# Input tiles of 96 neighbouring partitions, loaded ahead of the small constants, and one product of a step with 112 weight columns

## The chip, the cores and the metric

The kernel runs on one core of one Trainium2 chip, in float32. The metric is the device time of one execution in microseconds (us), as a median of several runs. The engines are TensorE (PE, with its weight loads listed as PEld), VectorE (DVE), ScalarE (ACT), GpSimd (POOL) and SyncE (SP, which here only issues DMA transfers).

## The reference

The input x has 32 images of 48 channels, 64 rows and 128 columns. Two layers follow one another. Each normalises x in 16 groups of three channels (GroupNorm without weights), passes the result through four recurrent scans, and adds x. A scan adds to each row (or column) a convolution of five taps of the row before it:

```python
def step(w, b):
    def f(carry, inp):
        nxt = inp + _conv1d(carry, w, b)      # 48 -> 48 channels, 5 taps
        return (nxt, nxt)
    return f
...
x = x + conv(_gn(x), down_w, down_b, right_w, right_b, left_w, left_b)   # twice
```

The first two scans run down and up the rows (both with the down weights), the last two right and left along the columns. Each step needs the one before it.

## The kernel before

**Groups and phases.** The 32 images are four groups of eight. A rows phase does the downward and upward scan of one group (126 steps), a columns phase the rightward and leftward scan of two groups (254 steps). There are twelve phases (PHASES) and 2024 steps, in one fixed order: rows of group 0, rows of group 1, columns of both, rows of group 2, and so on, for both layers.

**A step.** Eight neighbouring columns and 48 channels make 384 values, which lie as three blocks of 128 partitions (PIECES says which column offset e and which channels lie where). A row is then three blocks of 128 x 128 values: 16 column octets of eight images. The five taps reach from a block into the neighbouring ones, so a step is nine products (PRODUCTS, L63 to L73), of which two reach over the edge of an octet ("border" products, with 96 weight columns, BORDER). `step` (L710) issues them at L723; after the last product of a block the vector engine adds bias and input (L732) and so makes the next row. Each float32 product is two matmul records in the profile, so a step has 18.

**The order of work.** Every engine executes its instructions in the order in which the program issues them (`in_order`, L231). Around the steps, an agenda (`at`, L800) places other work at a step number: loads, row moves, scaling, statistics. `starts` holds the step at which each phase begins. What comes before the first step, and part of what runs during the first steps, is written out by hand in `first_group` (L1003 to L1129). All DMA transfers go out through `dma` (L226), on SP's queue if no other is given.

**Group 0's start.** `take_batch` loads x in two parts of rows, each part in a tile of 112 partitions: 48 channels of one run of 16 rows at partitions 0 to 47, 48 channels of the next 16 rows at partitions 64 to 111 (SIDES). The 16 partitions between are set to zero (L1035). Each image and side is a transfer of its own. From these tiles come three things:

- Statistics: DVE's bn_stats and bn_aggr (L395, L398), then in `scaling` (L289) products with a mask matrix that average over the three channels of a group and both sides (L300) and spread the result to the 128-partition layout (L311, with maskp), and the coefficients scale and offset (L351 to L374).
- Rows 0 to 7: `rows_by_product` (L1055) lets PE move the values into the three-block layout by products with pieces of an identity matrix (L1061); ACT copies the results out of PSUM (L1068). The identity pieces are cut from a tile in DRAM, `ident`, by small transfers into the space of the weights that are needed later.
- All other rows: `permute` (L544) rearranges a row of both sides on POOL (some quarters on ACT), `put_out` writes it to a DRAM tensor (xin), `move_rows` (L571) reads it back into the three-block layout, ten transfers for eight rows with runs of 128 bytes, and `scale_rows` (ACT, L596) or `scale_at_once` (DVE or POOL, L607) normalises it.

Between the loads of x, `let_go` mixes the small loads that were held back: the taps and weights (`load_weights`), the masks and biases (`load_constants`), and the identity pieces. `spread_masks` (L279) makes maskp and scales mask_in, which is used for the statistics of results later.

**Groups 1 to 3.** `plan_input` (L815) places the loads (`take_in`), permutes, puts and statistics (on ACT, `take_others`) of the other groups at steps of the agenda. Group 1's first load comes at the end of `first_group`, after the reads of group 0's rows. `plan_rows` (L835) places row moves and scalings.

Of the kernel before, what the change touches and what calls it, by code (L numbers as in the profile page):

```python
# [33 lines left out]
C = 48  # L34
ODD = 64
P = ODD + C
TAPS = 5
# [4 lines left out]
GB = 8  # L42
# [26 lines left out]
    (1, 2, 0),  # L69
    (0, 1, 0),  # L70
    (1, 1, 0),
    (2, 1, 0),
)  # L73
BORDER = 2 * C

# [43 lines left out]
def kernel(  # L119
# [57 lines left out]
    mask_sb = const([P, P], "mask_sb")  # L177
    maskp = const([P, NG, FULL], "maskp")
    mask_in = const([FULL, NG, P], "mask_in")
# [92 lines left out]

    def load_constants(dma):
        dma(mask_sb, mask)
        for e, c0, c1, o, p0 in PIECES:
            dma(bd[p0 : p0 + c1 - c0, o], bias[c0:c1])
            dma(mask_in[p0 : p0 + c1 - c0, o], mask[c0:c1])

    def spread_masks():  # L279
        for e, c0, c1, o, p0 in PIECES:  # L280
            nc.gpsimd.tensor_copy(maskp[:, o, p0 : p0 + c1 - c0], mask_sb[:, c0:c1])

        nc.gpsimd.tensor_scalar(mask_in, mask_in, 2.0 / E8, None, ALU.mult)
# [5 lines left out]
    def scaling(key, layer, g, averages, masks, slack=0):  # L289
# [29 lines left out]
        average(ps[0:P, 0], mean_p)  # L319
        if n == 1:  # L320
            expand(ps[:, 1 : 1 + NG], mean_p[:, 0])
# [3 lines left out]
        dev = spare[0 : FULL if n > 1 else P, 0:n]  # L325
        if n > 1:
            mean_c = stat_tile([P, GB], "mean_c", key)
            nc.vector.tensor_copy(mean_c, ps[0:P, 0])
            yield
            expand(ps[:, 1 : 1 + NG], mean_c)  # L330
            yield
            nc.vector.tensor_tensor(dev, mean_p, ps[:, 1 : 1 + NG], ALU.subtract)
        else:
            nc.vector.tensor_tensor(dev, mean_p, ps[0:P, 0:1], ALU.subtract)
        nc.vector.tensor_copy(mean, ps[:, 1 : 1 + NG])
        pool.tensor_tensor(dev, dev, dev, ALU.mult)
        yield
        for _ in range(slack):
            yield
        if n == 1:  # L340
            expand(ps[:, 2 + NG :], dev[:, 0], var_p[:, 0])
        else:
            average(ps[0:P, 1 + NG], dev, var_p)
            yield
            var_c = stat_tile([P, GB], "var_c", key)
            nc.vector.tensor_copy(var_c, ps[0:P, 1 + NG])
            yield
            expand(ps[:, 2 + NG :], var_c)
# [5 lines left out]
        nc.scalar.activation(std, var, AF.Sqrt)  # L354
        yield
        yield
# [20 lines left out]
    class InputStats:  # L377
# [3 lines left out]
        def __init__(self, key, nv):  # L381
            self.nv = nv
            self.mv = stat_tile([P, 1, GB, 2], "mv_x", key)
            if nv:
                self.st = stat_tile([P, nv, NBN * 6], "bn", key)
            if nv < GB:
                self.sum, self.neg, self.dev2 = (
                    stat_tile([P, GB, NBN], f"{n}_x", key)[:, nv:] for n in ("sum", "neg", "dev2")
# [11 lines left out]
        def take_others(self, i, nat):  # L400
            k = nat.shape[-1] // BN
            for square in (False, True):
                for b in range(self.nv, GB):
                    for n in range(k):
                        at = b - self.nv, slice(i + n, i + n + 1)
                        piece = nat[:, b, n * BN : (n + 1) * BN]
                        if square:
                            nc.scalar.activation(
                                junk[0:P],
# [5 lines left out]
                        else:  # L415
                            nc.scalar.activation(  # L416
                                junk[0:P],
# [8 lines left out]
        def __call__(self, key, slack):  # L426
# [3 lines left out]
            if self.nv < GB:  # L430
                n = GB - self.nv
                mean = stat_tile([P, GB], "mean_x", key)[:, 0:n]
# [6 lines left out]
                    dev, dev, mean.unsqueeze(2).to_broadcast([P, n, NBN]), ALU.add  # L439
# [7 lines left out]
                var = stat_tile([P, GB], "var_x", key)[:, 0:n]  # L447
# [74 lines left out]
    x_masks = [mask_sb]  # L522
    r_masks = [mask_in[:, g] for g in range(NG)]


    def take_in(g, h0, nat):

        n = nat.shape[-1] // W
        for s in range(2):
            h = h0 + s * n  # L530
            if n < E8:
                dma(
                    nat[SIDES[s]],
                    x[g * GB : (g + 1) * GB, :, h : h + n].rearrange("b c h w -> c b (h w)"),
                )
            else:
                for b in range(GB):
                    take_batch(g, b, h, s, nat)

    def take_batch(g, b, h, s, nat):  # L540
        n = nat.shape[-1] // W
        dma(nat[SIDES[s], b], x[g * GB + b, :, h : h + n].rearrange("c h w -> c (h w)"))
# [12 lines left out]
    def put_out(g, h, perm, stride):  # L555

        n = perm.shape[-1] // (W * GB)
        for s in range(2):
            dma(
                lines(source[0][g], h + s * stride, h + s * stride + n),  # L560
                perm[SIDES[s]].rearrange("p (m n) -> p m n", n=LINE),
            )
# [147 lines left out]
    def step(key, weights, b_at, src, inp, dst, whole, part):  # L710
# [8 lines left out]
        for i, o, s in PRODUCTS:  # L719
            seen[o] += 1  # L720
            m = BORDER if s else FULL
# [93 lines left out]
    def plan_input(g, times, work, lag, nats, perms):  # L815
# [5 lines left out]
        for j, t in enumerate(times):  # L821
# [3 lines left out]
            for i in range(per):  # L825
                perm, r = perms[i % len(perms)], i * rows // per
                at(t + i * work / per, permute, nat, r, perm, [nc.gpsimd])
                at(t + i * work / per + 4, put_out, g, 2 * rows * j + r, perm, rows)
            at(t + lag, stats.take_others, pieces_of * j, nat)
            if j + ahead < len(times):  # L830
                free = t + 7
                at(free, take_in, g, 2 * rows * (j + ahead), nat)
# [148 lines left out]
    def wide_nat(i0, n):  # L981
        return arena[0:P, i0 : i0 + GB * n * W].rearrange("p (b m) -> p b m", b=GB)

    tiles = [stage[0:P, i] for i in range(4)]
# [10 lines left out]

    at(starts[1] + 50, more_weights, "right", 0, RIGHT)
# [6 lines left out]
    def first_group():  # L1003
        later = []

        def hold(dst, src):
            later.append((dst, src))

        def let_go(n):
            for _ in range(min(n, len(later))):  # L1010
                dma(*later.pop(0))


        spare = {k: wt[k].rearrange("p i n -> p (i n)") for k in ("down1", "right", "left")}
        to_row = [spare["right"][0:C, i * FULL : (i + 1) * FULL] for i in range(9)]
        to_row += [spare["left"][0:C, 0:FULL]]
        one = last[0:C, 0 : C + 1]
        ident = dram.tile([C, C + 1], F32, tag="ident", name="ident")
        square = ident.rearrange("c n -> (c n)")[0 : C * C].rearrange("(c n) -> c n", n=C)

        def make_ident():
            dma(ident, one)
            for m, (e, c0, c1, o, p0) in zip(to_row, PIECES):
                hold(m[c0:c1, p0 : p0 + c1 - c0], square[c0:c1, c0:c1])
# [3 lines left out]
        nc.vector.memset(one, 0.0)  # L1028
        nc.vector.memset(one[:, 0:1], 1.0)
        for b in range(2 * GB):  # L1030
            if b == 2:
                nc.vector.memset(spare["right"], 0.0)
                nc.vector.memset(spare["left"], 0.0)
            i, b = divmod(b, GB)
            (nc.vector if b % 2 else nc.gpsimd).memset(parts[i][32:64, b], 0.0)  # L1035

        def take(i, b):
            for s in range(2):
                take_batch(0, b, i * HALF + s * rows, s, parts[i])

        stats = InputStats("x0", GB)
        perms = [spare["down1"][0:P, 0 : W * GB]]
        perms += [row_views(0)[0][0:P, o, 24:32].rearrange("p h n -> p (h n)") for o in range(NG)]
        more = [spare[k][0:P, 0 : W * GB] for k in ("down1", "right", "left")]
        more += [slot[2][0:P, i * W * GB : (i + 1) * W * GB] for i in range(4)]

        def permute_row(i, r, *engines):
            ring = more if i else perms
            permute(parts[i], r, ring[r % len(ring)], engines)

        def put_row(i, r):
            ring = more if i else perms
            put_out(0, i * HALF + r, ring[r % len(ring)], rows)

        def rows_by_product(h0, n):  # L1055
            src = parts[0][0:C].rearrange("p b (r k e) -> p e r k b", k=NK, e=E8)
# [16 lines left out]
        take(0, 0)  # L1073
        make_ident()
        for b in range(1, 3):
            take(0, b)
        load_weights("down0", 0, DOWN, hold)
        load_constants(hold)
        for b in range(3, GB):
# [125 lines left out]
```

## Time and profile before

| | |
|---|---|
| median of three runs | 4308.83 us (4308.38 to 4317.33) |
| profiled execution | 4311.88 us |
| its span in the profile | 4309.7 us |
| granted TensorE clock | 0.98 of full speed |
| first step starts at | 103.28 us |
| group 0's last row reads end at | 203.6 us |

A profile line of PE, DVE, ACT or POOL gives the line of the kernel, the engine, the operation, the output and input names, and the number of instructions, then their busy time and the mean of one in ns, then the idle time before them and what ended it. "L596 ... <-DMA arena<-xin 154.7" says that ACT's scaling at L596 stood idle for 154.7 us until DMA transfers from xin to the arena had landed. "SPq" is SP as the issuer of transfers. The page's costliest groups of instructions are, apart from the steps' products, ACT's row scaling (816 instructions, 576.0 us), POOL's permutes (458, 271.0 us at L553 into the arena) and the residual additions on POOL (80, 362.9 us). Over the whole span the DMA engines move 158 GB/s on average, 2,006,689 of 2,117,983 packets being under 512 bytes.

### The profile page before, as it was taken

What the parts mean: (1) busy time and instruction counts of PE and PEld (TensorE: products, weight loads), DVE (VectorE), ACT (ScalarE), POOL (GpSimd) and SP (SyncE); (2) the same over time, 40 slices, a digit from 0 to 9 for tenths busy, and PEclk for the clock granted to TensorE, in tenths of its full rate; (3) what the DMA queues carried; (4) which work ended last, traced back from release to release, by engine and by line L of the source; (5) the groups of instructions that cost most, each with busy time, mean ns of one, the idle gap of its engine ahead of it and who ended that gap; (6) DMA issues with size and microseconds to landing.
All of it is one profiled execution on the core that took longest, in us unless ns stands there. A gap on an engine that the chain in (4) does not pass through costs nothing. (4 is left out here: it accounts for less than half of the span.)

```text
span 4309.7 us, 90123 instructions
## 1 busy us (share of the span) xinstructions
PE 4080.8 (95%) x36672; PEld 4051.4 (94%) x36672; DVE 2161.1 (50%) x6508; ACT 1337.0 (31%) x2656; POOL 904.1 (21%) x906
## 2 busy tenths in 40 slices
PE   4898998999999999998999999999999999999992
PEld 1898998999999999998999999999999999999992
DVE  6344444446654454444446654444444444444443
ACT  1593301445784454200006772613000002110122
POOL 4571011325322020000005310000000024420352
PEclk9999999999999999999999999999999999999996
DMA  9999799877998999679507979929288039989999
GB/s 179 179 192 161 112 156 174 214 142 224 230 183 143 151 157 157 105 127 177 118 1 234 222 158 145 151 45 160 47 137 201 1 76 239 255 245 153 180 202 180
DMA packets 2117983, 680.34 MB, mean 158 GB/s; under 512 B 2006689, under 2 KB 2057409, under 8 KB 2077633
## 3 DMA queue, kind: packets, MB, share of 16 engines
q1 hardware_dynamic: 2019552, 582.30, 71.2%
q10 hardware_dynamic: 94816, 86.00, 9.9%
q0 software_dynamic: 3200, 6.30, 0.6%
q8 instruction: 288, 4.72, 0.5%
q14 instruction: 127, 1.03, 0.1%
HBM read 397.57 MB, written 295.99 MB: 161 GB/s over the span
## 5 line engine op out<-in xcount | busy, mean ns | idle before, releaser
L596 ACT ACTIVATE arena<-arena,offset,scale 128x256 f32<-128x256 f32 (+2 forms) x816 | 576.0, 799 | 399.2 <-DMA arena<-xin 154.7
L655 POOL TENSOR_TENSOR arena<-arena 128x2048 f32<-128x2048 f32 x80 | 362.9, 4550 | 1384.8 <-PE step_10l L723 473.2
L553 POOL COPY arena<-arena 112x256 f32<-112x256 f32 x458 | 271.0, 649 | 535.3 <-DMA arena<-in_x 404.6
L485 ACT ACTIVATE early<-arena 128x256 f32<-128x256 f32 x192 | 129.5, 674 | 455.6 <-DMA arena<-xin 319.9
L723 PE MATMUL step_01r<-arena,early 128*128 128x128 f32 x2286 | 251.6, 274 | 16.0 <-DMA arena<-upa 16.0
L723 PEld LDWEIGHTS step_01r<-arena,early 128*128 128x128 f32 x2286 | 251.4, 187 | 16.3 <-issue 16.2
L723 PE MATMUL step_00r<-arena,early 128*128 128x128 f32 x2286 | 251.3, 273 | 16.2 <-DMA arena<-upa 16.2
L723 PEld LDWEIGHTS step_00r<-arena,early 128*128 128x128 f32 x2286 | 251.0, 187 | 16.6 <-issue 16.6
L723 PE MATMUL step_11r<-arena,early 128*128 128x128 f32 x2286 | 252.6, 274 | 5.5 <-DVE arena L732 5.5
L723 PEld LDWEIGHTS step_11r<-arena,early 128*128 128x128 f32 x2286 | 252.1, 187 | 5.9 <-DVE arena L732 5.8
L723 PE MATMUL step_00l<-arena,wleft 128*128 128x128 f32 x2286 | 249.6, 272 | 0.0
L723 PE MATMUL step_10r<-arena,early 128*128 128x128 f32 x2286 | 249.3, 272 | 0.0
L723 PEld LDWEIGHTS step_10r<-arena,early 128*128 128x128 f32 x2286 | 249.1, 186 | 0.2 <-DVE arena L732 0.2
L723 PEld LDWEIGHTS step_00l<-arena,wleft 128*128 128x128 f32 x2286 | 249.2, 186 | 0.0
L723 PE MATMUL step_10l<-arena,wleft 128*128 128x128 f32 x2286 | 249.1, 272 | 0.0
L723 PE MATMUL step_11l<-arena,wleft 128*128 128x128 f32 x2286 | 249.1, 272 | 0.0
L723 PE MATMUL step_01l<-arena,wleft 128*128 128x128 f32 x2286 | 249.1, 272 | 0.0
L723 PEld LDWEIGHTS step_10l<-arena,wleft 128*128 128x128 f32 x2286 | 249.0, 186 | 0.0
L723 PEld LDWEIGHTS step_11l<-arena,wleft 128*128 128x128 f32 x2286 | 249.0, 186 | 0.0
L723 PEld LDWEIGHTS step_01l<-arena,wleft 128*128 128x128 f32 x2286 | 249.0, 186 | 0.0
L680 ACT COPY arena<-arena 128x256 f32<-128x256 f32 x172 | 99.6, 655 | 415.7 <-POOL arena L655 153.7
L416 ACT ACTIVATE early<-arena 112x512 f32<-112x512 f32 x192 | 121.1, 631 | 299.0 <-DMA arena<-in_x 232.0
(188 smaller groups left out, 7094.4 us busy)
## 6 DMA issues: line engine op xcount, KB each, us to landing
arena<-in_x SPq DMA_DIRECT2D x48, 768.0 KB, 12.6
xin<-arena SPq DMA_DIRECT2D x96, 384.0 KB, 5.7
arena<-xin SPq DMA_DIRECT2D x96, 384.0 KB, 8.3
mid<-arena SPq DMA_DIRECT2D x96, 384.0 KB, 7.7
arena<-mid SPq DMA_DIRECT2D x192, 192.0 KB, 4.2
upb<-arena SPq DMA_DIRECT2D x192, 192.0 KB, 3.9
arena<-upb SPq DMA_DIRECT2D x96, 384.0 KB, 11.8
arena<-xin SPq DMA_DIRECT2D x186, 192.0 KB, 4.2
```

Of the source, the lines that this page charges most:

```text
L416: nc.scalar.activation(junk[0:P], piece, AF.Identity, accum_out=self.sum[:, at[0], at[1]],)
L485: nc.scalar.activation(junk[:, 0:n], view[:, b], AF.Identity, accum_out=self.sum[:, i, j : j + 1])
L553: copy(dst[:, r, q], src[:, r0 + r, q])
L596: nc.scalar.activation(args[0], args[0], AF.Identity, bias=args[2], scale=args[1])
L655: eng.tensor_tensor(unit, unit, nat, ALU.add)
L680: copy(by_w(perm)[:, a], src[:, a])
L723: nc.tensor.matmul(part(whole(ps[o])[0:m], -s), weights[:, i, at : at + m], part(src(i), s), start=seen[o] == 1, stop=seen[o] == left[o],)
```

## The change

There are six edits.

1. The product (0, 1, 0) gets 112 weight columns instead of 128 (COLUMNS). It changes places with (1, 1, 0), which is now the first product of block 1.
2. x is loaded to 96 partitions without a gap, channel by channel with its two sides as neighbours (partition 2c + s). The sides are the two halves of the image: part 0 of group 0 holds rows 0 to 15 and 32 to 47, part 1 rows 16 to 31 and 48 to 63. One transfer carries both sides, so group 0 has 16 loads instead of 32. The memsets of the gap go. Masks, statistics and identity pieces follow the new order of partitions; a put takes every second partition.
3. All 16 loads of x are issued first on SP. The weights of group 0 (5 taps, 25 pieces) and the constants (2 mask, 10 bias) go out on ACT's queue (`aside`). The ten loads of mask_in move to 58 steps into the second phase, and their scaling, now two POOL instructions (`spread_row_masks`), to 90 steps into it.
4. The identity pieces are made by ten affine_select instructions on POOL instead of eleven transfers.
5. In `scaling`, for x the products that spread the mean come after the root is issued, and the variance is added to the squared deviation on DVE, so that one product per block spreads both. `scale_at_once` does row 0 alone, then rows 1 to 3.
6. The hand-written order of permutes, puts and reads changes, with new rings of buffers; spread_masks now stands ahead of the permutes of rows 12 to 15.

The core of the diff:

```diff
-    (0, 1, 0),
     (1, 1, 0),
+    (0, 1, 0),
     (2, 1, 0),
 )
 BORDER = 2 * C
+COLUMNS = {(0, 2, 1): BORDER, (2, 0, -1): BORDER, (0, 1, 0): FULL - C // 3}
...
-            m = BORDER if s else FULL
+            m = COLUMNS.get((i, o, s), FULL)
...
+    def take_in(g, r0, nat, batches=slice(0, GB)):
         n = nat.shape[-1] // W
...
+        src = x[g * GB : (g + 1) * GB].rearrange("b c (s h) w -> (c s) b (h w)", s=2)
+        dma(nat[:, batches], src[:, batches, r0 * W : (r0 + n) * W])
...
-    def put_out(g, h, perm, stride):
+    def put_out(g, r, perm):
         n = perm.shape[-1] // (W * GB)
         for s in range(2):
+            h = s * HALF + r
             dma(
-                lines(source[0][g], h + s * stride, h + s * stride + n),
-                perm[SIDES[s]].rearrange("p (m n) -> p m n", n=LINE),
+                lines(source[0][g], h, h + n),
+                sided(perm)[s].rearrange("p (m n) -> p m n", n=LINE),
             )
```

In `scaling` (pool is DVE for group 0):

```diff
-        average(ps[0:P, 0], mean_p)
-        if n == 1:
-            expand(ps[:, 1 : 1 + NG], mean_p[:, 0])
+        average(ps[0:PX, 0], mean_p)
...
         pool.tensor_tensor(dev, dev, dev, ALU.mult)
+        if n == 1:
+            pool.tensor_tensor(dev, dev, var_p, ALU.add)
...
-            expand(ps[:, 2 + NG :], dev[:, 0], var_p[:, 0])
+            expand(ps[:, 2 + NG :], dev[:, 0])
...
         nc.scalar.activation(std, var, AF.Sqrt)
+        if n == 1:
+            expand(ps[:, 1 : 1 + NG], mean_p[:, 0])
         yield
+        if n == 1:
+            nc.vector.tensor_copy(mean, ps[:, 1 : 1 + NG])
```

In `spread_masks`, and in the agenda:

```diff
+        for s in range(2):
+            nc.gpsimd.tensor_copy(mask_x.rearrange("p (c s) -> p s c", s=2)[:, s], mask_sb)
         for e, c0, c1, o, p0 in PIECES:
             nc.gpsimd.tensor_copy(maskp[:, o, p0 : p0 + c1 - c0], mask_sb[:, c0:c1])
-        nc.gpsimd.tensor_scalar(mask_in, mask_in, 2.0 / E8, None, ALU.mult)
...
+    at(starts[1] + 58, load_row_masks)
+    at(starts[1] + 90, spread_row_masks)
```

In `first_group`, after the change (permute_rows, put_rows: rows r0 to r1 of part i through a ring of buffers; free, late and later have seven, six and five buffers):

```python
def aside(dst, src):
    dma(dst, src, nc.scalar)
...
for i in range(2):
    for b in range(GB):
        take_in(0, i * rows, parts[i], slice(b, b + 1))
nc.vector.memset(spare["right"], 0.0)
nc.vector.memset(spare["left"], 0.0)
load_weights("down0", 0, DOWN, aside)
load_constants(aside)
make_ident()
for b in range(GB):
    stats.take(0, parts[0], b)
permute_rows(0, 8, 12, free, nc.gpsimd, nc.scalar)
put_rows(0, 8, 12, free)
rows_by_product(0, 4)
spread_masks()
permute_rows(0, 12, 15, free, nc.gpsimd, nc.scalar)
put_rows(0, 12, 15, free)
permute_rows(0, 15, 16, free, nc.gpsimd)
put_rows(0, 15, 16, free)
rows_by_product(4, 4)
for b in range(GB):
    stats.take(NBN // 2, parts[1], b)
    stats.aggregate(b)
move_rows(0, 8, 16, False)
for r in range(0, 8, 2):
    permute_rows(1, r, r + 2, free, nc.gpsimd)
    put_rows(1, r, r + 2, free)
for _ in scaling("x0", 0, 0, stats, x_masks):
    pass
scale_at_once(0, 0, 1, nc.vector)
scale_at_once(0, 1, 4, nc.vector)
scale_rows(0, 4, 8)
scale_rows(0, 8, 16)
move_rows(0, 16, 24, False)
scale_rows(0, 16, 24)
permute_rows(1, 8, 12, late, nc.gpsimd)
put_rows(1, 8, 12, late)
permute_rows(1, 12, 16, late, nc.gpsimd)
put_rows(1, 12, 16, late)
move_rows(0, 24, 32, False)
scale_rows(0, 24, 32)
permute_rows(0, 0, 4, later, nc.gpsimd)
put_rows(0, 0, 4, later)
permute_rows(0, 4, 8, later, nc.gpsimd)
put_rows(0, 4, 8, later)
move_rows(0, 32, 48, False)
...
```

Before the change, the permutes ran in the order: rows 8 to 15 of part 0, rows 0 to 7 of part 0, rows 0 to 3 of part 1, reads of rows 16 to 32, then rows 4 to 15 of part 1, with the gap memsets, the identity transfers and the held-back small loads ahead of and between the loads of x.

## The prediction

> **What bounds the kernel now.** I read the page's busy shares first, then PE's waits, then windows of the first 350 us, and last the instructions by shape.
>
> ```profile
> PE 4080.8 (95%) x36672; PEld 4051.4 (94%) x36672; DVE 2161.1 (50%) x6508; ACT 1337.0 (31%) x2656; POOL 904.1 (21%) x906
> ```
>
> TensorE is busy for 95% of the span, and no other engine for more than half. So time can be saved in two ways: cheaper products, or fewer of the 4309.7 - 4080.8 = 229 us in which PE has nothing to do. PE's waits name these:
>
> ```profile
> PE rows L1061 <- DMA arena<-in_x: 38.7, 1, 38.7
> ...
> PE ps_x L300 <- DVE mv_x_x L398: 15.0, 1, 15.0
> PE step_00d L723 <- DVE arena L732: 14.9, 4, 10.3
> PE step_01d L723 <- DVE arena L732: 13.0, 2, 12.3
> PE step_00d L723 <- DVE arena L607: 7.6, 1, 7.6
> ```
>
> Columns: total us, times, longest. The first, second and last lines lie before the first step, which starts at 103.28 us: the load of x, the statistics after it, the first scaling. In the step_00d line group 0 waits for rows 16 and 32, in the step_01d line group 1 for its row 16. There DVE is only the messenger: its addition waits for ACT's scaling of rows, and that for the row reads.
>
> The windows show what fills this time (columns: busy us of PE, PEld, DVE, ACT, POOL with counts; clock, DMA share, GB/s):
>
> ```profile
> 0.00:40.00 40.00, 1.27 (x2) 0.72 (x3) 33.12 (x40) 0.00 (x0) 15.26 (x13) 1.00 0.93 171
> 40.00:60.00 20.00, 20.00 (x23) 6.72 (x23) 12.78 (x22) 7.49 (x12) 5.52 (x10) 1.00 1.02 215
> 60.00:88.00 28.00, 15.46 (x17) 4.72 (x16) 10.06 (x19) 3.04 (x4) 10.05 (x25) 1.00 0.77 154
> 88.00:103.00 15.00, 4.55 (x20) 4.37 (x20) 9.70 (x18) 3.35 (x9) 10.25 (x17) 1.00 0.99 173
> 103.00:138.00 35.00, 34.72 (x288) 34.65 (x288) 14.75 (x46) 20.21 (x44) 32.51 (x56) 1.00 0.86 187
> 138.00:204.00 66.00, 51.06 (x422) 50.27 (x421) 23.39 (x72) 48.04 (x94) 14.92 (x26) 0.90 0.99 185
> 3275.00:3300.00 25.00, 25.00 (x232) 25.00 (x231) 12.26 (x39) 0.00 (x0) 0.00 (x0) 1.00 1.01 334
> ```
>
> The DMA engines are at 93 to 102% of their time with only 171 to 215 GB/s, while the last line, a spill of 128-partition tiles, moves 334 GB/s at the same share. So the load occupies the engines without their full rate. Up to 204 us the chain is: load, statistics, coefficients, and beside these row permutes on POOL, their puts to DRAM, reads back, ACT scaling.
>
> **What the Trainium skill says.** "SBUF — State Buffer", section "Door 1: The DMA port swizzle": partitions 0 to 63 lie on eight of sixteen ports, 64 to 127 on the other eight. A 48-partition load at 0 or at 64 thus reaches eight, one over partitions 0 to 95 all sixteen, the first eight with twice the bytes. The trace agrees on the slow side: an 8 KB packet of the 48-partition loads takes 689 ns on average, one of the spill 391 (309 at the tenth percentile). No transfer on 96 partitions is in the trace. "DMA: Bandwidth & Descriptors", section "Issuing engines are not separate DMA queues": loads issued by ACT save sequencer time, not transfer. "TensorE: Matmul & The Clock Gate", section "LDWEIGHTS (loading the stationary operand)": time goes by columns, one in 1/1.2 ns. The trace agrees:
>
> ```profile
> L723 PEld LDWEIGHTS step_11r<-arena,early 128*128 128x128 f32 x1778 | 211.1, 193 | 5.9 <-DVE arena L732 5.8
> L723 PEld LDWEIGHTS step_11r<-arena,early 128*96 128x96 f32 x508 | 60.0, 165 | 0.0
> ```
>
> (193 - 165)/32 = 0.88 ns per column.
>
> **The change, part by part.**
>
> *112-column product.* Two of a step's 18 matmul records get 112 weight columns. The start-to-start time of unstalled records is 111.7 ns with 128 columns and 128 moving, 102.5 with 96 and 120, 95.8 with 96 and 112. These fit the larger of (moving/1.2 + 2.5) and (next load's columns/1.2 + 5): the product goes from 111.7 to 109.2, where the moving side takes over. 2 x 2.5 x 2024 steps = 10 us. The other end is the start-to-start time of a 96-column load followed by a 128-moving product, 110.9: 2 x 0.75 x 2024 = 3 us. Stalled steps absorb a little: I take 9. The order swap inside the step costs nothing: the two products write different banks, and block 1 still finishes before block 2.
>
> *Load of x.* Now 12.6 MB in 32 transfers share the queue with small loads: part 0 lands at 38.7, the last batch at 87.5. After: 16 transfers at the head of SP's queue. Bounds on the rate: 191 (the present packet time) and 334 GB/s (all ports). The uneven halves put it between; I take 260. 786 KB then take 3.0 us: part 0 at 2.5 + 24 + about 6 for issue to landing = 33 (24 to 38), all x at about 56 (44 to 70). The gap memsets (14.0 us on POOL, 14.1 on DVE) and eleven identity DMAs go; ten POOL selections, 0.2 to 0.7 us each by the rows for POOL copies, run during the load. DVE needs 2.47 us per batch, under the arrival interval, so statistics end about 61.
>
> *What is late next.* The rows by product: from 38.73 to 75.5 (40 x 0.91 us) PE builds rows 0 to 7, at present before x is complete. After, it runs 35 to 72, past the statistics' 61, and becomes the bound. From there PE's average, DVE, PE, ACT, DVE: today 90.46 to 99.77, less 1.4 for six expansions moved behind the root and about 1.4 for variance expansions saved, plus 0.2 for the addition: 6.8, so offsets at 79. Scaling row 0 alone costs about 1 of today's 3.5 us. First step: 80, against 103.3: **23 us**.
>
> *Small loads on ACT.* 42 issues on ACT at 0.6 to 1.0 us are 25 to 42 us (SP's puts take 0.76 us, its reads about 1 us an issue). They hide under the load: ACT's first need is the permutes of rows 8 to 12 at 33, then the PSUM copies (L1068) at 41. But SP's and ACT's DMAs draw from one ring of eight completion semaphores in program order, and each waits for the one eight before it: in the trace of before the two queues alternate on the same eight at 668 us, and SP waited 28.5 us for in_x in 21 waits. If several small DMAs are dealt between two loads of x, ACT is free at E = 36. Dealt one to one, its tail waits for the last of x and E is 62 to 68. Behind it stand the permutes, the mask and the copies that free PSUM for PE's second half (18 us): PE then ends at E + 20 and the first step is at E + 28. I take 36 as likelier.
>
> *Row chain.* POOL permutes (2.36 us per row), puts and reads (ten per eight rows, about 10 us) keep their number. What they run against is the DMA engines: to 88 us these moved 171 x 40 + 215 x 20 + 154 x 28 KB = 15.4 MB (GB/s by us), of it 12.6 of x. After: 3 us to the first packet, 12.6 MB at 260 in 48, the other 2.8 MB at the 215 of the second window in 13: 64, or **24 us** earlier. From 88 to the end of group 0's reads (203.6) the DMA share is 0.86 to 0.99 and the work is the same, so reads end at about 180. Row 16 is read after 16 permutes instead of 20, row 24 after 24 instead of 20, row 32 after 32 as before. The stalls at rows 16 and 32 (17.0 and 10.4 us) stay on the whole, as the first step and the reads move together (23 and 24). Group 1's loads start where group 0's reads end; its row 16 now leaves PE free at 428, after 24 us earlier. Group 1's own load also needs less DMA time, 12.6 MB at 260 instead of 191, 18 us less; ACT paces that stretch (eight tiles of statistics at 13 us each), so I count none.
>
> *Mask loads and spread_row_masks.* Ten SP issues at step 184 and two POOL operations of about 1 us at step 216 lie beside steps; first use is a result's statistics, over 250 steps on. Nothing; at most 10 us of SP queue ahead of the column reads if that cover is thin. spread_masks (1.6 us) and two copies more go in front of POOL's permutes of rows 12 to 15: 2 us in their chain, under the wait for the DMA engines. Queued behind a late mask it holds up all later permutes; that is the bad case above. For groups 1 to 3 half as many input loads are issued: nothing.
>
> Sum: 24 + 9 = 33 against the profiled run, 4311.88 (span 4309.7 and 2.2 around it), which gives 4279; against the median 4308.83, 3 less: **4276**.
>
> **Rivals.**
> 1. *The row chain gains more* (20%): the 18 us of group 1's load count too, since the DMA share from 203 to 430 is 0.96 to 0.98, and the product gives its 10: 24 + 18 + 10 = 52: 4257. Against: ACT's pace.
> 2. *ACT held by the ring* (15%): E = 65, first step at 93, chain gains 10: 10 + 9 = 19: 4290.
> 3. *No faster transfer* (8%): x at 191 GB/s takes 66 us, with the 13 and 3 above 82 against 88; chain gains 6, product 3: 4300. For it: no such transfer in the trace.
> 4. *Slower* (7%): the ring, worse. The weights wait for their taps and these for loads of x, the copies and the mask come later, POOL's stream stands behind spread_masks. First step at E + 28: it decides from E = 75. At 85 the first step is at 113 and reads end 10 later: +10 - 3 = 7 later: 4316.
>
> **How the numbers follow.** Likeliest case 50% (4266 to 4286), rivals 20, 15, 8, 7. About 0.2%, 8.6 us, is what a measurement of this kernel can tell from no change: below 4300.2 counts as faster. Faster: 50 + 20 + 15 + 2 = 87; same 7; slower 6. Range 4250 to 4302: it takes in rival 1's better half, rival 2 and rival 3, and leaves out the slower one.
>
> **What would show it.** Right: in_x packets well under 689 ns and over 230 GB/s in the first 50 us; PE's wait for in_x 31 to 35 instead of 38.7; the wait at L300 for L398 gone, as rows by product ends after the statistics; first step near 80; group 1's stall at row 16 ending about 24 earlier; 112-column loads near 179 ns (halfway from 165 to 193), unstalled steps 5 ns shorter. Wrong: ACT's PSUM copies starting after 60, PE waiting for them, a first step over 95, or steps at rows 16 and 32 that stall 20 us longer than now.

## The result, and the profile after

The changed kernel takes 4292.39 us (median of 20 runs) against 4308.37 for the kernel before (20 runs). The medians lie 16 us apart, the means (4293.9 and 4307.2) 13 us. The ratio follows the means: 0.9969 of the kernel before, interval 0.9959 to 0.9979, that is 13 us less (9 to 18). The forecast was 33 us less. The profiled execution's span is 4288.2 us against 4309.7.

The busy shares after the change, then PE's longest waits (total us, times, longest):

```profile
PE 4058.9 (95%) x36648; PEld 4029.3 (94%) x36648; DVE 2164.5 (50%) x6503; ACT 1340.1 (31%) x2662; POOL 886.2 (21%) x906
```

```profile
PE rows L1074 <- DMA arena<-in_x: 41.7, 1, 41.7
PE step_00d L741 <- DVE arena L750: 31.7, 6, 14.9
PE step_00d L741 <- DVE arena L625: 24.7, 1, 24.7
PE step_01r L741 <- DMA arena<-upa: 14.4, 1, 14.4
```

PE now waits longer for x than before (41.7 against 38.7 us). The wait at L300 for the statistics is gone, as forecast, but the wait for the first scaling has grown from 7.6 to 24.7 us, and that for rows of group 0 from 14.9 to 31.7. The first step starts at 107.83 us, 4.5 us later than before. The windows of the start (columns as before):

```profile
0.00:40.00 40.00, 0.00 (x0) 0.00 (x0) 19.32 (x30) 1.28 (x1) 2.92 (x15) 1.00 0.68 167
40.00:60.00 20.00, 18.34 (x20) 6.38 (x21) 16.65 (x29) 5.70 (x10) 10.09 (x26) 1.00 1.02 260
88.00:103.00 15.00, 0.00 (x0) 0.00 (x0) 15.00 (x1) 0.00 (x0) 15.00 (x27) 1.00 0.95 216
103.00:138.00 35.00, 27.25 (x216) 26.77 (x217) 18.77 (x45) 31.20 (x67) 6.66 (x9) 0.95 0.16 26
```

Three things stand out. In the first 40 us the DMA engines work only 0.68 of the time, though half of x is still to be loaded; from 40 to 60 they run at 260 GB/s, the rate that was forecast. From 88 to 103 DVE shows one single instruction (x1) that is busy for all 15 us, while POOL is busy throughout. From 103 to 138 the DMA engines are nearly idle (0.16), though the puts and reads of rows are still to be done.

The single DVE instruction is the first product of the coefficients, 128 x 24 elements, with both operands in SBUF. The timeline shows it beside POOL's permutes (start, duration, engine, line; POOL's lines follow):

```profile
83.25 0.29 DVE L387 RECIPROCAL std_x<-std_x 128x24 f32<-128x24 f32 x1
83.58 22.07 DVE L389 TENSOR_TENSOR dev_x<-var_x,std_x 128x24 f32<-128x24 f32 x1
105.68 0.18 DVE L390 TENSOR_TENSOR dev_x<-dev_x,std_x 128x24 f32<-128x24 f32 x1
```

```profile
75.72 13.83 POOL L569 COPY arena<-arena 96x256 f32<-96x256 f32 x24
89.49 2.35 POOL L569 COPY early<-arena 96x256 f32<-96x256 f32 x4
91.79 2.35 POOL L569 COPY wleft<-arena 96x256 f32<-96x256 f32 x4
94.08 6.93 POOL L569 COPY arena<-arena 96x256 f32<-96x256 f32 x12
100.96 4.64 POOL L569 COPY early<-arena 96x256 f32<-96x256 f32 x8
108.37 4.05 POOL L569 COPY wleft<-arena 96x256 f32<-96x256 f32 x4 [2.77 <-DMA xin<-wleft]
```

POOL copies without a pause from before L389 starts until 105.6, and L389 ends at 105.65. The same instruction (then L362) took 2.13 us before the change. There too it ended when POOL paused (98.66), but it came near the end of POOL's run:

```profile
91.72 6.94 POOL L553 COPY arena<-arena 112x256 f32<-112x256 f32 x12
96.57 2.13 DVE L362 TENSOR_TENSOR dev_x<-var_x,std_x 128x24 f32<-128x24 f32 x1
```

For the idle DMA engines, SP's waits between 100 and 220 us after the change:

```profile
SPq L231 <- ACT arena L614: 44.5, 2, 34.8
SPq L231 <- DMA xin<-arena: 2.6, 1, 2.6
```

SP stands for 34.8 us at one put of a permuted row until ACT has scaled other rows, and for 9.7 us at a second. Before the change SP never waited for ACT between 100 and 240 us; most of its waiting there was for POOL's permutes:

```profile
SPq L227 <- POOL arena L553: 24.0, 11, 12.7
```

The last read of group 0's rows is issued at 225.2 us, against 203.6 before and 180 in the forecast.

### The profile page after: what moved, and what is told of

The parts are those of the page before. It is cut to its first block, busy times and chain, and to the rows that moved or that the text cites. A ratio compares the mean times of both kernels' runs of the same rounds, so it can differ in the third digit from the quotient of the medians.

```text
span 4288.2 us, 89979 instructions
## 1 busy us (share of the span) xinstructions
PE 4058.9 (95%) x36648; PEld 4029.3 (94%) x36648; DVE 2164.5 (50%) x6503; ACT 1340.1 (31%) x2662; POOL 886.2 (21%) x906
## 5 line engine op out<-in xcount | busy, mean ns | idle before, releaser
L569 POOL COPY arena<-arena 96x256 f32<-96x256 f32 x448 | 265.0, 650 | 553.8 <-DMA arena<-in_x 444.2
## 6 DMA issues: line engine op xcount, KB each, us to landing
arena<-mid SPq DMA_DIRECT2D x192, 192.0 KB, 4.2
upb<-arena SPq DMA_DIRECT2D x192, 192.0 KB, 3.9
arena<-xin SPq DMA_DIRECT2D x186, 192.0 KB, 4.3
```

The costliest lines, as they stand in the source:

```text
L569: copy(dst[:, r, q], src[:, r0 + r, q])
```

## The experiments

Ratios are to the kernel before, measured beside it on the same chip; runs whose labels begin with the same letter share that measure. The theory after the result (A): three separate losses at the start, namely puts that wait for ACT without need, VectorE held by POOL, and loads of x held by small loads. The rivals are named with each run. A step's start is the start of its first matmul record; steps are counted from 0, and step k of the first scan makes row k + 1.

### VectorE and POOL

**e1: POOL pauses for the coefficients.**

```diff
-        for r in range(0, 8, 2):
-            permute_rows(1, r, r + 2, free, nc.gpsimd)
-            put_rows(1, r, r + 2, free)
         for _ in scaling("x0", 0, 0, stats, x_masks):
             pass
         scale_at_once(0, 0, 1, nc.vector)
         scale_at_once(0, 1, 4, nc.vector)
+        nc.gpsimd.tensor_copy(junk[:, 0:1], row(0, 3)[:, 0, 0:1])
+        for r in range(0, 8, 2):
+            permute_rows(1, r, r + 2, free, nc.gpsimd)
+            put_rows(1, r, r + 2, free)
```

> Edit: the permutes of part 1's rows 0 to 7 come after the coefficients and row 0 to 3's scaling, and a one-element POOL copy makes POOL wait for these. Theory A (VectorE's product of two SBUF operands, 22.07 us at L389 in the changed kernel against 0.18 elsewhere, cannot start while POOL copies one after the other): that instruction falls to under 1 us, the first step starts at 86 to 89 instead of 107.8. POOL's 16 rows start some 12 us later, so rows 16 to 24 are read at about 115 and SP's wait for ACT ends near 132 instead of 140.8: 5 to 12 us faster than the changed kernel, 4280 to 4287. Theory B (what the start lost is the load: part 0 at 41.6 and the last batch at 66 instead of 33 and 56, and the rest is hidden by the DMA engines): within 4 us of the changed kernel's 4292.

Measured: 0.9969 (0.9959 to 0.998), the changed kernel's ratio. In the profile L389 takes 0.18 us and the first step starts at 85.7, so VectorE was indeed held by POOL. But the steps then stand still for 22.6 us at row 4, because ACT's first scaling waits 27.28 us for puts of other rows:

```profile
108.92 21.25 ACT L614 ACTIVATE arena<-arena,offset,scale 128x64 f32<-128x64 f32 x47 [27.28 <-DMA xin<-arena]
```

Step 4 starts at 118.1 us, against 117.4 in the changed kernel. 22 us at the first step were worth nothing at the end: here theory A missed the time, and theory B's number came true.

**f11 and g4: a PSUM operand in every product of the chain** (on top of f1, below). f11 without the last hunk:

```diff
+            t0 = ps[:, 2 + 2 * NG : 2 + 3 * NG]
+            nc.vector.scalar_tensor_tensor(
+                t0, ps[:, 2 + NG : 2 + 2 * NG], GN_EPS, r0, ALU.add, ALU.mult
+            )
...
-        scale_at_once(0, 0, 1, nc.vector)
+        scale_at_once(0, 0, 1, nc.vector, "first")
...
-        pool.tensor_tensor(offset, mean, scale, ALU.mult)
-        pool.tensor_scalar(offset, offset, -1.0, None, ALU.mult)
+            nc.vector.scalar_tensor_tensor(
+                offset, ps[:, 1 : 1 + NG], -1.0, scale, ALU.mult, ALU.mult
+            )
```

("first" are copies of scale and offset in PSUM; the deviation is squared through PSUM too.)

> As f1, and group 0's coefficients are worked out with one operand in PSUM in each product (copies of scale and offset in PSUM serve row 0 to 3's scaling). Theory A (VectorE waits for POOL only when both operands lie in SBUF): no instruction of the coefficient chain over 1 us while POOL copies, first step at 86 to 89 instead of 97 to 108. But ACT's first scaling still waits for the puts of part 1's rows 0 to 7, which read every second partition and stand ahead of it, until 95 to 100, so the steps stall at rows 4 and 8: 0 to 8 us faster than f1. Theory D (VectorE is held by POOL whatever the operands): the first step stays at 97 to 108.

> As f11, and the sign of the offset goes into the product with the mean, so that no VectorE instruction from the deviation to the scaling of rows 0 to 3 has all its operands in SBUF. Theory A: none of them over 1 us while POOL copies without a pause (in f11 the one left, L417, took 10.01), first step at 85 to 88 against 96.9 in f1. ACT's scaling still starts at 95 to 98, so the steps wait for rows 4 to 8: 0 to 8 us faster than f1. Theory D (VectorE is held whatever the operands): some instruction of the chain takes 5 us or more again.

Measured: f11 0.9887 (0.9868 to 0.9905), g4 0.9883 (0.9868 to 0.9898), both within f1's interval (0.9861 to 0.9898). In f11 the products no longer wait, and the one operation left with SBUF on both sides, a sign change, waits instead, so that the first step still starts at 96.2:

```profile
84.46 0.18 DVE L414 TENSOR_TENSOR offset<-ps_x,scale 128x24 f32<-128x24 f32 x1
84.68 10.01 DVE L417 TENSOR_SCALAR offset<-offset 128x24 f32<-128x24 f32 x1
```

In g4 that one is gone too, and the chain runs through while POOL copies 24 pieces without a pause:

```profile
84.64 0.19 DVE L403 TENSOR_TENSOR ps_x<-ps_x,std_x 128x24 f32<-128x24 f32 x1
85.09 0.18 DVE L412 TENSOR_TENSOR scale<-std_x,ps_x 128x24 f32<-128x24 f32 x1
85.30 0.18 DVE L414 SCALAR_TENSOR_TENSOR offset<-ps_x,scale 128x24 f32<-128x24 f32 x1
```

```profile
77.61 13.92 POOL L592 COPY arena<-arena 96x256 f32<-96x256 f32 x24
```

g4's first step starts at 87.2, against 96.9 in f1. Theory D falls. For L389 this is what the Trainium skill says in "SBUF — State Buffer", section "Who interferes with whom": a DVE instruction with two SBUF inputs contends with a GpSimd instruction that reads SBUF. I had not used it in the forecast. L417 has only one such input and was held too, so that sentence alone doesn't cover it.

### Puts and ACT

**e2, e3, f1: later rings outside the arena.** e2 changes the rings alone, e3 adds e1's pause; f1 also takes the rows in pairs (e2 and e3 put a later row's values into the first of each four rows, so f1's time is the one that counts).

```diff
-        late = wide + free[4:7]
-        later = wide + [stage[0:PX, 3, i * n : (i + 1) * n] for i in range(2)]
+        late = wide
+        later = wide
...
-        permute_rows(1, 8, 12, late, nc.gpsimd)
-        put_rows(1, 8, 12, late)
-        permute_rows(1, 12, 16, late, nc.gpsimd)
-        put_rows(1, 12, 16, late)
+        for r in range(8, 16, 2):
+            permute_rows(1, r, r + 2, late, nc.gpsimd)
+            put_rows(1, r, r + 2, late)
...
```

> Edit: the two later rings of buffers are cut to the three weight tiles, so no put after the first scaling reads from the arena tile. Theory A (SP's 34.8 and 9.7 us waits for ACT at L614 come from puts that read every second partition of the arena while ACT scales other rows of it): both waits vanish, the puts of rows 24 to 31 go out from 106 on, the stalls at steps 23 and 31 (15.8 and 17.0 us) fall under 5 each, the reads of group 0 end 25 to 35 us earlier than 215: 4260 to 4272. The first step stays at 107 to 109. Theory B (load): the rings of three make POOL wait for puts instead, within 4 us of 4292.

> Both edits. Theory A: first step at 86 to 89, no wait of SP for ACT, reads of group 0 end at 165 to 180: 4250 to 4268. Theory B: within 6 us of 4292.

> As e2 (later rings only in the weight tiles), with permutes and puts in pairs of rows, so that with three buffers no row is overwritten before it is put out; in e2 and e3 groups of four permutes preceded their puts, and the first row of each four carried a later row's values. Theory A: the time of e2, 0.988 to 0.992 of the kernel before. Rival (e2 was fast because its puts were mixed up): 0.996 or above.

Measured: e2 0.99 (0.9883 to 0.9918), e3 0.9932 (0.9913 to 0.9951), f1 0.988 (0.9861 to 0.9898). SP's waits for ACT are gone and the last read of group 0 is issued at 193.3 us in f1. e2's first step came earlier than expected, at 97.0: POOL now pauses at 94.8, when its three buffers are full, and lets L389 through after 10.61 us. f1 shows the same (10.60). e3's first step is early (86.3), but after the pause POOL takes up its rows at 89.7 instead of 74.1, and the time is worse than e2's and between the two theories.

**f4: sides on neighbouring partitions.** It keeps the rings in the arena and changes which partitions a put reads, at the price of two loads of 48 partitions (masks and identity pieces follow the new order).

```diff
-        return t.rearrange("(c s) n -> s c n", s=2)
+        return t.rearrange("(s c) n -> s c n", s=2)
...
-        src = x[...].rearrange("b c (s h) w -> (c s) b (h w)", s=2)
-        dma(nat[:, batches], src[:, batches, r0 * W : (r0 + n) * W])
+        src = x[...].rearrange("b c (s h) w -> s c b (h w)", s=2)
+        for s in range(2):
+            dma(nat[s * C : (s + 1) * C, batches], src[s, :, batches, r0 * W : (r0 + n) * W])
...
```

> Edit: the two sides lie on partitions 0 to 47 and 48 to 95 without interleaving, so x comes by two loads of 48 partitions again, and each put reads 48 neighbouring partitions; rings, order and the rest as changed. Theory A (the waits between puts and ACT's scaling come from the partition step of two): SP never waits for ACT at L614 after 100 us, though the rings still use the arena, stalls at steps 23 and 31 under 6 us each. The loads run at 170 to 200 GB/s, last x at 75 to 90, so the first step is at 100 to 112. 0.989 to 0.994 of the kernel before. Rival (the waits come from the rings' place in the arena): SP's waits of some 35 and 10 us stay, 0.997 or above.

Measured: 0.9904 (0.9885 to 0.9923). SP's longest waits after 100 us in f4:

```profile
SPq L231 <- DVE arena L751: 6.5, 7, 3.2
SPq L231 <- POOL early L570: 6.5, 6, 1.5
```

ACT's scaling is not among them, although the buffers lie where they lay. So the wait needs a source that steps over every second partition, and the rival falls; f1 shows that it also needs a source in the arena. The rows that ACT scales (16 to 23) and the buffer that SP puts out (the space of rows 24 to 31) share no element, so it is a wait that the assignment of waits adds, not one that the data need; that it takes such a source for more of the tile than it reads is inferred. The loads of 48 partitions, with small loads between them, brought part 0 at 48.2 us (136 GB/s in the first 40 us), later than in any other kernel, and still the time is 0.65% under the changed kernel's. Part of that may be VectorE's: in f4 L389 took 0.29 us beside POOL, and the first step starts at 95.3.

### Small loads

**f5, g1, g2: weights, masks and biases on POOL's queue**, with the identity pieces made first; alone (f5), with f1 (g1), with f4 (g2).

```diff
+        make_ident()
         load_weights("down0", 0, DOWN, aside)
         load_constants(aside)
-        make_ident()
...
-            dma(dst, src, nc.scalar)
+            dma(dst, src, nc.gpsimd)
```

> Edit: weights, masks and biases of group 0 go out on POOL's queue instead of ACT's, after the identity pieces. Theory A (the loads of x wait for small loads with which they share eight completion semaphores): SP issues x without gaps, part 0 lands at 28 to 34 instead of 41.6, the last batch at 54 to 60 instead of 66, DMA share over 0.9 in the first 40 us. POOL's 42 issues hold its permutes back until 45 to 60; with SP's waits for ACT unchanged the time is within 8 us of the changed kernel, 0.996 to 0.999. Rival (x was slow for its 96 partitions): part 0 stays at 38 to 44.

> f1 and f5 together: later rings in the weight tiles, puts in pairs, small loads on POOL's queue. Theory A (the early load is worth its 20 to 30 us only if the puts and ACT's scaling don't wait for each other): first step at 74 to 90, no wait of SP for ACT at L614 after 60 us; ACT's first scaling still waits for the puts of part 1's rows 0 to 7. 0.981 to 0.986 of the kernel before, that is 8 to 25 us faster than f1's 0.988. Rival (the row chain is bound by the DMA engines and POOL): within 5 us of f1.

> f4 and f5 together: sides on partitions 0 to 47 and 48 to 95, two loads each, rings as changed, small loads on POOL's queue. Theory A: without small loads between them the 48-partition loads run at 180 to 210 GB/s, part 0 lands at 34 to 38, the last x at 64 to 70; no false wait is left; first step at 80 to 92; 0.983 to 0.988. Rival (loads of 48 neighbours are as fast as those of 96 when they lie back to back): part 0 at 28 to 31 as in f5.

Measured: f5 0.9932 (0.9907 to 0.9957), g1 0.9881 (0.9868 to 0.9895), g2 0.9899 (0.9884 to 0.9914). f5's first window, to be held against 0.68 and 167 GB/s in the changed kernel:

```profile
0.00:40.00 40.00, 11.47 (x13) 4.22 (x14) 29.75 (x48) 6.36 (x10) 19.22 (x47) 1.00 0.98 251
```

Part 0 lands at 28.5, the last load of x is issued at 28.4 instead of 42.2, the first step starts at 75.3. An 8 KB packet takes 499 ns on average between 5 and 40 us, nearly the 512 of the changed kernel: the loads were not slow, they were issued late. SP's waits in the first 60 us of the changed kernel name the small loads that held them, 30 us in all:

```profile
SPq L231 <- DMA early<-taps: 11.9, 3, 6.2
SPq L231 <- DMA bd<-in_b: 10.0, 2, 7.7
SPq L231 <- DMA taps<-in_w: 8.2, 1, 8.2
```

There the transfers of SP and ACT count on the same eight completion semaphores: the third load of x, at 9.82 us, waits for the one that the fifth load of taps had been given. In f5 SP and POOL have eight each, and none of these three waits is left. In g2 part 0 lands at 34.5 and the first window shows 204 GB/s, so 96 partitions are worth about 47 GB/s over two times 48, and the rival of g2 falls; its time still missed the 0.983 to 0.988 of theory A. In f5 SP's waits for ACT remain (32.4 us in two), and the gain of 32 us at the first step is 21 at step 250. Only some 14 of the 32 come from the load: L389 took 0.29 us in f5 instead of 22.07. f5's time is better than the 0.996 to 0.999 expected: by the ratios it is 16 us under the changed kernel's, with some 12 us of uncertainty, although the puts still waited. g1 missed its expectation: by the ratios it is within its rival's 5 us of f1.

### The product

**e4: the changed kernel with 128 columns again; g3: the kernel before with 112 columns.**

```diff
-COLUMNS = {(0, 2, 1): BORDER, (2, 0, -1): BORDER, (0, 1, 0): FULL - C // 3}
+COLUMNS = {(0, 2, 1): BORDER, (2, 0, -1): BORDER, (0, 1, 0): FULL}
```

> Edit: the product (0, 1, 0) back to 128 weight columns, all else as changed. Theory A: unstalled steps 4.9 ns longer, 2024 of them: 10 us slower than the changed kernel, 4302. Theory C (the product's gain is taken up by stalls): under 4 us slower.

> The kernel before with the 112-column product and the new order of products, nothing else. Theory A: unstalled steps 4.9 ns shorter, 2024 of them: 10 us faster than the kernel before, 0.9972 to 0.9982 of it. Theory C (stalls take it up): under 4 us, 0.999 or above.

Measured: e4 0.998 (0.9973 to 0.9987), where e1 on the same chip and the changed kernel have 0.9969; g3 0.999 (0.998 to 1.0). Both speak for 4 to 5 us, between theories A and C, each with 4 to 5 us of uncertainty, so they lie as far from nothing as from 9. The steps themselves are as forecast: the new load in the changed kernel is

```profile
L741 PEld LDWEIGHTS step_11r<-arena,early 128*112 128x112 f32 x254 | 36.8, 179 | 0.0
```

and the median step takes 1975 ns in rows (1980 before) and 1955 in columns (1960), 5 ns less from start to start. 2024 times 5 ns are 10.1 us. The profiled executions show the gain where few steps wait for loads: from step 758 to the last step, 2023, pass 2532.4 us before and 2533.8 in e4, but 2518.0 to 2527.4 in the 16 other profiles, all with 112 columns; 1265 times 5 ns would be 6.3.

### All on one chip

**h1: the changed kernel. h2: f1. h3: f1 with g4's chain and f5's queue. h4: g1 with part 1's rows 0 to 7 in the weight tiles too** (`free` becomes `wide` in their permutes and puts).

> The changed kernel itself, as the measure for the three beside it on the same chip. All theories: 0.996 to 0.998 of the kernel before.

> f1 again on this chip. Theory A: the false waits of the puts are worth 30 to 42 us, 0.987 to 0.990. Rival: under 20 us.

> f1 with small loads on POOL's queue and the coefficients with a PSUM operand: all three lost terms of the start mended. Theory A: first step at 72 to 78; ACT's first scaling still waits for part 1's first puts until 92 to 98, so of the 20 us by which the first step is earlier than in f1 5 to 15 are left: 0.984 to 0.987. Theory E (once the puts are free of false waits, the DMA engines and ACT set the end, and an earlier first step is worth nothing): within 4 us of h2.

> g1 with part 1's rows 0 to 7 in the weight tiles too, so that no put that comes after the load of x's second part reads the arena. Theory A: ACT's first scaling starts with the coefficients, at 72 to 80 instead of about 93, and the stalls at rows 4 to 8 fall by 10 us or more; three buffers in place of seven slow the permutes of these rows. 0.983 to 0.988. Theory E: within 4 us of h2.

| | first step | last read of group 0 issued | median us | ratio (interval) |
|---|---|---|---|---|
| before | 103.3 | 203.6 | 4305.27 | |
| h1 | 108.9 | 226.6 | 4291.11 | 0.9973 (0.9962 to 0.9984) |
| h2 | 96.4 | 192.0 | 4258.96 | 0.9896 (0.988 to 0.9912) |
| h3 | 72.8 | 183.2 | 4254.32 | 0.9887 (0.9873 to 0.9902) |
| h4 | 73.6 | 189.9 | 4257.46 | 0.9892 (0.9879 to 0.9905) |

h2 is 0.9973 - 0.9896 = 0.77% faster than h1, 33 us (about 25 to 41). This is put to the puts' false waits, though h2's rings also let VectorE in earlier and start the steps 12 us sooner: where the first step alone came earlier (e1 against the changed kernel by 22 us, g4 against f1 by 10) no gain showed. With the false waits gone, a first step 24 us earlier (h3 against h2) brings the last read forward by 8.8 us, and the steps of the profiles stay some 8 us ahead from step 64 (233.6 against 242.0) to the last (4168.9 against 4176.2). The medians lie 4.6 us apart, and the intervals allow from 5 us slower to 13 faster. So h3 and h4 missed the ratios of theory A, and the times do not tell A's 5 to 15 us from E's 4; the profiles show that about a third of the earlier start arrives. PE's waits in h3 show where the first step's gain goes:

```profile
PE rows L1097 <- DMA arena<-in_x: 28.6, 1, 28.6
PE step_00d L764 <- DVE arena L773: 25.3, 5, 13.1
PE step_01r L764 <- DMA arena<-upa: 13.8, 1, 13.8
...
PE step_00d L764 <- DVE arena L648: 3.2, 1, 3.2
```

13 us less wait for x than in the changed kernel and 21.5 less for the first scaling, but 25.3 us at group 0's later rows, against 11.8 in h2. In h4 ACT starts early, and the stall moves on to rows 16, 24 and 32. h2, h3 and h4 all beat both kernels; h3 has the lowest median.

## Why the prediction was wrong

**Load of x.** The rate was right (260 GB/s in the second window; taken: 260). The times were not: part 0 at 41.7, not 33; the last batch's statistics began at 66.4, not at 56. I had costed the shared completion semaphores in one direction only, ACT waiting for x. ACT was free at 36.6, as taken; SP's loads waited for ACT's small ones. f5 shows it: part 0 at 28.5, even under my 33. So rival 2 named the right place and the wrong queue; its 4290 is near the result by accident.

**The chain to the first step.** The change's savings came, but the step "from 72 to 79, 6.8 us" failed. From the end of the rows by product at 78.2 to the offsets at 106.7 it took 28 us, 22.07 of them in L389. The profile of before held the sign: 2.13 us for 128 x 24 elements where its neighbours took 0.18. I counted these 2.13 as the cost of the operation instead of asking what it waited for. The new order of permutes gave POOL a run long enough to turn 2 us into 22.

**Row chain.** This was the dearest step. I took the row chain to run against the DMA engines alone: "the work is the same, so reads end at about 180". They ended at 225, because two puts that read the arena by every second partition waited 34.8 and 9.7 us for ACT's scaling. Where ACT was ready sooner, it waited in turn for such puts (27.28 us in e1). f4 (no step over partitions) and f1 (no arena) both remove SP's waits; h2 against h1 sizes the loss at about 33 us. I had read what is moved, but not which instructions a changed access makes dependent on each other.

**Loads of the later groups.** Group 1's was counted at none, in rival 1 at 18. From the last read of group 0 to the first read of group 1 passed 203.6 to 338.3, 134.7 us, before; 225.2 to 339.9, 114.7, after; 115.8 in h3 (183.2 to 299.0). In f4, with loads of 48, it is 122.6 (195.5 to 318.1). So some 20 us were gained there, about 8 of them by the 96 partitions; the rest comes with the new order and wasn't taken apart. For groups 2 and 3 the prediction said "nothing". But group 2's rows (steps 506 to 632) took 268.9 us before and 260.0 after. In the 14 profiles with loads of 96 partitions they took 259.9 to 266.8, in the four without (the kernel before, g3, f4, g2) 268.9 to 273.4. That the loads do this is read from this order alone; no run isolates it.

**The product.** Its step is right (5 ns); its share in the end, put at 9, is 4 to 5 us by the times, with an uncertainty as large.

**Sum.** The starts of the steps in the profiled executions show where the time went (us against the kernel before; minus is earlier):

| start of step | 0 | 23 | 33 | 126 | 252 | 506 | 632 | 758 | 2023 | span |
|---|---|---|---|---|---|---|---|---|---|---|
| changed kernel | +4.5 | -5.4 | +21.6 | +18.2 | +0.4 | +0.1 | -8.8 | -12.1 | -18.8 | -21.5 |
| h1 (the same kernel) | +5.7 | -2.5 | +23.6 | +19.7 | +0.9 | +0.8 | -8.3 | -12.8 | -20.3 | -20.5 |
| h3 | -30.5 | -26.4 | -19.6 | -23.3 | -41.5 | -42.2 | -45.5 | -47.7 | -55.5 | -55.5 |

In the changed kernel the row chain's 24 us turned into a loss of 18 by the end of group 0's rows (step 126). Group 1's rows (126 to 252) won 18 back, so up to step 506 nothing was gained at all. What the change is worth came afterwards: 9 us in group 2's rows, 3 in the next phase, 7 from step 758 to the last, where the product alone would give 6, and 3 behind the last step. So none of the result comes from the start, on which 24 of the forecast's 33 us rested. The largest part comes from a term that had been put at nothing, and that it and group 1's rows made up for the start was luck. The faster load and the shorter chain do appear once nothing stands in their way. In h3, with the three losses mended, part 0 is at 28.6 (33 forecast), the first step at 72.8 (80), and the last read at 183 (180). Step 126 comes 23 us earlier (24 forecast), and group 1's rows add 18, as in rival 1; h3's median is 51 us under the kernel before, where rival 1 said 52.

## What to carry to other kernels

A transfer that is made cheaper by another layout also changes what it is ordered against: look at the waits of each instruction that touches the new access, above all where scratch buffers share a tile with live data. Before a producer on POOL is moved up beside a short VectorE chain, give the chain one operand in PSUM; a pause of POOL also let the chain through here, but it delayed POOL's own rows (e1, e3). And an early start is worth only what the next resource lets through: of 24 us at the first step about 8 were left from step 64 on.

## What the runs showed of the hardware

VectorE's request lost to POOL not for one instruction, but for as long as POOL had the next one ready: 22.07 us over some 38 POOL instructions. It is not chance of one run: the changed kernel, profiled a second time, shows 23.22 (h1), and f1 and h2, one kernel, both 10.60. In f5 the same chain beside the same copies waited for one POOL instruction at a time:

```profile
70.24 0.29 DVE L389 TENSOR_TENSOR dev_x<-var_x,std_x 128x24 f32<-128x24 f32 x1
70.57 0.54 DVE L390 TENSOR_TENSOR dev_x<-dev_x,std_x 128x24 f32<-128x24 f32 x1
71.14 0.53 DVE L392 TENSOR_SCALAR dev_x<-dev_x 128x24 f32<-128x24 f32 x1
```

L389 started 391 ns into a POOL copy in the changed kernel and 388 ns into one in f5, so the moment of the request does not tell the cases apart. Nor does the kernel: L357 and L359 of the changed kernel, with both inputs in SBUF, got in after 0.44 and 0.54 us beside the same stretch of copies, 4 us before L389. What does tell them apart is open. A 128 x 24 product with an operand in PSUM took 0.18 to 0.19 us beside POOL in every case. A 96-partition load of 8 KB packets ran at 250 to 260 GB/s, between the 204 of 48-partition loads (g2) and the 334 of the 128-partition spill before.

The granted TensorE clock fell to half during the longest stalls: in the changed kernel from 165.8 to 179.4 us, while step 23 stood from 159.8 to 175.6, and from 196.5 to 213.6, with step 31 from 191.6 to 208.6. The steps right after, 24 and 32, took 4.2 and 4.5 us instead of 2.0. So each of these two stalls cost some 2 us more than it lasted. In e1, whose steps also stand still at row 4, the clock was at half from 99.3 to 123.2 us too, and its mean clock is 0.978 against 0.981.
